# Four gates' 1x1 convolutions as one group of 16 small products, with mixing tiles shared by four gates

## The chip, the cores and the metric

The kernel runs on one core of a Trainium2 chip. The metric is the time of one launch on the device in microseconds (us). TensorE (PE in the profile) multiplies matrices into PSUM; VectorE (DVE), ScalarE (ACT) and GpSimd (POOL) do elementwise work; SyncE (SP) and GpSimd issue DMA transfers. Each engine has a queue of its own and takes its instructions in the order of the program.

## The reference

The input is x of 8 batch elements, 8 channels, 512 x 512, in float32. Two layers follow one another, each added to its own input. The second one, cut to what matters here:

```python
def layer0(x):                    # on group-normalized x: 4 x 8 Fourier modes
    ...
def _L1_conv_ref(x, ...):         # on group-normalized x
    grid = drive = x
    for _ in range(15):
        mapped = 3.9 * grid * (1.0 - grid)
        local = conv3x3_per_channel(mapped, K_local)
        grid = 0.85 * (0.7 * mapped + 0.3 * local) + 0.15 * drive
    cml_out = clip(grid, 0.0001, 0.9999)
    h = relu(conv3x3(x, Wp, bp))                      # 8 -> 128 channels
    nca_out = sigmoid(conv1x1(h, Wu, bu))             # 128 -> 8
    gin = concat([x, cml_out, nca_out], axis=1)       # 24 channels
    g = sigmoid(conv1x1(relu(conv3x3(gin, Wg1, bg1)), Wg2, bg2))
    return g * cml_out + (1.0 - g) * nca_out
```

The change concerns the last two lines, the gate: a 3x3 convolution from 24 to 8 channels, a 1x1 from 8 to 8, and the mixing.

## The kernel before

All batch elements go through one core, one after another, in a program written out by hand: `keep_order` fixes the order of the source on every engine. The loop works in turns (`turn`, `work`). A turn holds, for element b:

- two of the 15-step map's slots (`Slabs.convolve` L524 and `settle` L537/L543). A slab holds 4 x 32 rows of 4 channels; one step is 48 products of 32x32 tiles into a pair of PSUM tiles, two adding instructions on VectorE (L537) and two squares on ScalarE (L543). Its row renewals (L570, L571) are DMAs issued by GpSimd.
- up to two hidden rounds (`Hidden.round` L723), each four rows of the 3x3 into 128 channels, evicted by ScalarE (L729) and VectorE (L731); after two rounds the 1x1 of the hidden layer (`Hidden.point` L742) with the eviction of y (L749 on ScalarE or L751 on VectorE), and after four a sigmoid (L755) and a store of 16 rows.
- `Others`: the gates of element b - 1, and the spectral layer (layer 0) of element b + 1, in pieces.

PSUM is four tiles, `pairs`, of two banks each. A turn's `near` and `far` are two pairs each: the first slot and the first round use near, the second ones far, and the gate's and the hidden layer's products at the end of the turn use near again. After two rounds the list of pairs is reversed, so the next turn's first slot uses what was far.

A gate (`Gate`) is 12 rows of output; an element has 43. `load` brings `gin` (three DMAs of 384, 320 and 320 KB) and `mix` (three of 192 KB). `conv` (L793) is 12 products into one bank. GpSimd takes the difference d of map and hidden output (L798), VectorE adds the scaled input (L799) and evicts with relu (L803). One turn later `point` does the 1x1 as three products of 128x32 weights in another bank (L810), ScalarE the sigmoid (L814), GpSimd the product with d (L816). One more turn later `finish` adds on VectorE (L821) and stores (L828). Its call stands after each slot's adding instructions.

Tiles for gates and spectral inputs come from 20 slots of 1 MB that they share with the map (`Slots`); `shared.most` bounds how many they may hold: 5, or 8 in the first part of an element, or 3 around the middle and the end. In `feed`, which runs between the slots and the rounds of a turn, gates are loaded, up to two ahead, with two slots each; the spectral layer keeps up to four.

After the last element's loop a tail remains: that element's other 80 hidden rounds and its 43 gates, one a turn.

Of the kernel before, what the change touches and what calls it, by code (L numbers as in the profile page):

```python
# [35 lines left out]
F32 = mybir.dt.float32  # L36
# [30 lines left out]
AHEAD, PAUSE = 12, 6  # L67
# [50 lines left out]
def conv_layers(ctx: ExitStack, tc: tile.TileContext, a, out):  # L118
# [10 lines left out]
    class Slots:  # L129
# [16 lines left out]

        def drop(self, t):
            self.free.append(self.held.pop(id(t))[1])
# [47 lines left out]
    gpoint = load("w_g2", [P, GR * C])  # L196
# [118 lines left out]
    def layer0(e, bank):  # L315
# [89 lines left out]
        def close(g, mv):  # L405
# [4 lines left out]
            for c in (2 * g, 2 * g + 1):  # L410
# [3 lines left out]
                def store(c=c, xt=xt):  # L414
                    nc.sync.dma_start(
# [349 lines left out]
    class Gate:  # L765


        def __init__(self, e, first):
            self.e, self.first, self.r0 = e, first, min(first, N - GR)

        def load(self):

            r0, self.at = self.r0, now[0]
            self.gin = shared.take([P, 4, N], "gin")
            self.mix = shared.take([P, 4, N], "mix")
            for q, src in enumerate((self.e.xn, self.e.cml, self.e.nca)):
# [3 lines left out]
                    in_=view(src, r0 * C * N, [[N, rows * C], [3 * C * N, 4], [1, N]]),  # L780
                )
            for q, src in enumerate((self.e.xn, self.e.cml, self.e.nca)):
                nc.sync.dma_start(
                    out=self.mix[: GR * C, q],
                    in_=view(src, (r0 + 1) * C * N, [[N, GR * C], [1, N]]),
                )

        def conv(self, ps):

            gin, (x1, d, ng) = self.gin, (self.mix[: GR * C, q] for q in range(3))  # L790
            for n, (dx, lo, hi, at) in enumerate(SHIFTS):
                for j in range(4):
                    nc.tensor.matmul(  # L793
                        ps[32 * j : 32 * j + 32, lo:hi], gband[:, dx], gin[:, j, at : at + hi - lo],
                        start=(n == 0), stop=(n == 2), tile_position=(0, 32 * j),
                    )

            nc.gpsimd.tensor_tensor(d, d, ng, ALU.subtract)  # L798
            nc.vector.scalar_tensor_tensor(  # L799
                x1, x1, self.e.back[: GR * C, 1:2], ng, ALU.mult, ALU.add  # L800
            )
            shared.drop(gin)
            nc.vector.tensor_scalar(self.mix[:, 3], ps, b_g1, 0.0, ALU.add, ALU.max)  # L803

        def point(self, ps):
            mix = self.mix
            ps = ps[: GR * C]
            for j in range(3):
                at = slice(32 * j, 32 * j + 32)
# [339 lines left out]
```

## Time and profile before

| | |
|---|---|
| Median of 3 runs | 9484.28 us (9464.85 to 9497.41) |
| Profiled execution, its own time | 9485.99 us |
| Its span, first to last instruction | 9484.2 us |
| Mean granted TensorE clock | 0.985 |
| L524, the map's products | 103680 records, 3696.7 us busy |
| L793, the gates' 3x3 | 8256 records, 963.8 us busy in two rows of the table by form |
| L814 sigmoid | 344 x 677 ns |
| L798, L816 on GpSimd | 344 x 1290 and 344 x 1274 ns |
| L799, L821, L803 on VectorE | 344 x 954, 921 and 750 ns |

A matrix product in float32 shows as two records of a matmul and two of a weight load, so twice as many records as products stand in the profile. The time between the starts of two groups tells what a group costs TensorE, since records overlap. A row of the table of costliest groups gives line, engine, operation, output and input tiles, shapes and count; then busy time and the mean of one in ns; then how long the engine sat idle just before them, and what ended that.

### The profile page before, as it was taken

What the parts mean: (1) busy time and instruction counts of PE and PEld (TensorE: products, weight loads), DVE (VectorE), ACT (ScalarE), POOL (GpSimd) and SP (SyncE); (2) the same over time, 40 slices, a digit from 0 to 9 for tenths busy, and PEclk for the clock granted to TensorE, in tenths of its full rate; (3) what the DMA queues carried; (4) which work ended last, traced back from release to release, by engine and by line L of the source; (5) the groups of instructions that cost most, each with busy time, mean ns of one, the idle gap of its engine ahead of it and who ended that gap; (6) DMA issues with size and microseconds to landing.
All of it is one profiled execution on the core that took longest, in us unless ns stands there. A gap on an engine that the chain in (4) does not pass through costs nothing. (4 is left out here: it accounts for less than half of the span.)

```text
span 9484.2 us, 331791 instructions
## 1 busy us (share of the span) xinstructions
PE 9052.0 (95%) x148976; PEld 4062.8 (43%) x148976; DVE 5647.2 (60%) x5820; ACT 4078.4 (43%) x4285; POOL 3362.1 (35%) x4422
## 2 busy tenths in 40 slices
PE   6999999999999999999999999999999999988998
PEld 3444444444444444444444444444444444333433
DVE  5665566655665556655566555665566655545555
ACT  2444444444444444444444444444444444434432
POOL 3232334334333343433434343243433433444322
PEclk9999999999999999999999999999999999999999
DMA  4241365555655655655655556565575665675287
GB/s 151 83 128 37 95 170 138 144 138 141 154 151 140 142 132 147 166 132 133 158 134 161 144 118 169 126 162 141 117 181 134 162 138 125 144 164 132 65 207 192
DMA packets 698558, 1327.07 MB, mean 140 GB/s; under 512 B 146938, under 2 KB 152442, under 8 KB 669650
## 3 DMA queue, kind: packets, MB, share of 16 engines
q1 hardware_dynamic: 594432, 1249.10, 52.1%
q0 software_dynamic: 100352, 55.61, 2.9%
q8 instruction: 1171, 19.19, 0.9%
q14 instruction: 249, 2.04, 0.1%
q10 hardware_dynamic: 2354, 1.14, 0.0%
HBM read 977.48 MB, written 270.61 MB: 132 GB/s over the span
## 5 line engine op out<-in xcount | busy, mean ns | idle before, releaser
L524 PE MATMUL pair<-m,band 32*32 32x512 f32 x103680 | 3696.7, 603 | 164.2 <-issue 105.7
L543 ACT ACTIVATE m<-m 128x1024 f32<-128x1024 f32 x2016 | 2128.5, 1056 | 2425.9 <-DVE m L537 2358.8
L723 PE MATMUL pair<-cols,w_p 32*128 32x511 f32 (+1 forms) x24576 | 2854.9, 603 | 59.8 <-DVE m L537 16.4
L524 PEld LDWEIGHTS pair<-m,band 32*32 32x32 f32 x103680 | 1999.4, 103 | 1793.0 <-issue 1006.5
L570 POOL DMA_DIRECT2D m<-m x1568 | 864.1, 551 | 3929.1 <-ACT m L543 3853.4
L537 DVE SCALAR_TENSOR_TENSOR m<-pair,dO 128x1024 f32<-128x1024 f32 x1152 | 1356.6, 1220 | 1187.3 <-PE pair L524 1023.6
L723 PEld LDWEIGHTS pair<-cols,w_p 32*128 32x128 f32 x24576 | 1302.0, 186 | 1627.7 <-issue 1147.9
L537 DVE SCALAR_TENSOR_TENSOR m<-pair,dE 128x1024 f32<-128x1024 f32 x1008 | 1187.8, 1220 | 1106.6 <-PE pair L524 912.8
L731 DVE TENSOR_SCALAR h<-pair,b_p 128x1024 f32<-128x1024 f32 x1024 | 1313.3, 1283 | 870.2 <-PE pair L723 865.3
L729 ACT ACTIVATE h<-pair,b_p 128x1024 f32<-128x1024 f32 x1024 | 1141.4, 1115 | 894.4 <-PE pair L723 893.7
L742 PE MATMUL pair<-h,w_u 128*32 128x512 f32 x8192 | 1062.7, 611 | 42.4 <-ACT h L729 40.8
L793 PE MATMUL pair<-gin,w_g 128*32 128x511 f32 (+1 forms) x8256 | 963.8, 600 | 3.7 <-DMA gin<-nca 2.9
L816 POOL TENSOR_TENSOR mix<-mix 96x512 f32<-96x512 f32 x344 | 438.3, 1274 | 1336.2 <-ACT mix L814 1267.7
L571 POOL DMA_DIRECT2D m<-m x1568 | 844.9, 539 | 30.0 <-issue 25.9
L742 PEld LDWEIGHTS pair<-h,w_u 128*32 128x32 f32 x8192 | 245.2, 110 | 699.8 <-issue 347.3
L755 ACT ACTIVATE y<-y,b_u 128x512 f32<-128x512 f32 x256 | 185.1, 723 | 821.8 <-DVE y L751 821.8
L793 PEld LDWEIGHTS pair<-gin,w_g 128*32 128x32 f32 x8256 | 234.8, 110 | 683.0 <-issue 458.1
L798 POOL TENSOR_TENSOR mix<-mix 96x512 f32<-96x512 f32 x344 | 443.8, 1290 | 73.2 <-DMA mix<-nca 69.1
L547 POOL TENSOR_SCALAR dO<-dO 128x2048 f32<-128x2048 f32 x72 | 391.9, 5443 | 112.4 <-DVE m L537 111.4
L749 ACT COPY y<-pair 128x512 f32<-128x512 f32 x256 | 150.2, 587 | 637.8 <-PE pair L742 510.2
L516 POOL TENSOR_SCALAR dO<-dO,base 128x512 f32<-128x512 f32 x288 | 207.1, 730 | 580.8 <-DMA dO<-xn 502.6
L810 PE MATMUL pair<-mix,w_g 128*32 128x512 f32 x2064 | 370.3, 605 | 42.7 <-DVE mix L803 39.6
(89 smaller groups left out, 3280.9 us busy)
## 6 DMA issues: line engine op xcount, KB each, us to landing
gin<-xn SPq DMA_DIRECT2D x344, 384.0 KB
cols<-xn SPq DMA_DIRECT2D x256, 512.0 KB
x<-in_x SPq DMA_DIRECT2D x120, 1024.0 KB
gin<-cml SPq DMA_DIRECT2D x344, 320.0 KB
gin<-nca SPq DMA_DIRECT2D x344, 320.0 KB
dE<-xn SPq DMA_DIRECT2D x288, 256.0 KB
dO<-xn SPq DMA_DIRECT2D x288, 256.0 KB
mix<-xn SPq DMA_DIRECT2D x344, 192.0 KB
```

The lines of the kernel that those rows point to most:

```text
L524: nc.tensor.matmul(ps[h // 2][32 * t : 32 * t + 32, h % 2], band[at, self.channel(step - 1, h, t), dx], m[at, t, dx : dx + N], start=(n == ...
L537: nc.vector.scalar_tensor_tensor(u[:, at], ps[q], FLOOR, d[:, at], ALU.max, ALU.add)
L543: nc.scalar.square(u[:, at], u[:, at])
L570: nc.gpsimd.dma_start(out=view(tb, rb, dims), in_=view(ta, ra, dims))
L571: nc.gpsimd.dma_start(out=view(ta, ra + s, dims), in_=view(tb, rb + s, dims))
L723: nc.tensor.matmul(ps[g // 2][:, g % 2, lo:hi], w_p[p, dx, i % 2], self.cols[p, i // 2, at : at + hi - lo], start=(n == 0), stop=(n == 2), ...
L729: nc.scalar.activation(h[:, :2], ps[0], AF.Relu, bias=b_p)
L731: nc.vector.tensor_scalar(h[:, 2:], ps[1], b_p, 0.0, ALU.add, ALU.max)
L742: nc.tensor.matmul(ps[32 * g : 32 * g + 32], w_u[:, r % 4], h[:, g], start=(r == self.hs[0][0]), stop=(r == self.hs[-1][0]), tile_position ...
L793: nc.tensor.matmul(ps[32 * j : 32 * j + 32, lo:hi], gband[:, dx], gin[:, j, at : at + hi - lo], start=(n == 0), stop=(n == 2), tile_positi ...
L798: nc.gpsimd.tensor_tensor(d, d, ng, ALU.subtract)
L816: nc.gpsimd.tensor_tensor(d, d, mix[: GR * C, 2], ALU.mult)
```

## The change

Four gates make a `Quad`; eleven of them an element, the last of three gates. The four gates' 3x3 go one a turn as before, each with its own `gin` tile, but the four column groups of gate k are rotated by k (`to`), so that the relu results of four gates lie in different partitions; they are evicted into one tile `relu`, which takes the place of the first gate's `gin` (`swap`). The three mixing inputs are tiles `ng`, `d` and `x1` that all four gates share, of 128 partitions (four groups of 32, of which 24 hold results) and four gates; they are loaded once the fourth gate's `gin` has been, as slots come free, by 12 DMAs of 256 KB.

`blend` does the mixing for the four at once: one subtraction on GpSimd and two instructions on VectorE. `point` does the 1x1 of the four gates as 16 products of 32x32 weights, each in a tile of the array of its own, into all four banks of near; then two sigmoids on ScalarE and two multiplications on VectorE (on GpSimd before). `finish` adds half a quad at each call, so over two slots, and the quad is stored at the end of the turn by 12 DMAs.

`feed` moves from between the slots and the rounds to the end of the turn; loading the spectral input stays where it was (`fetch`). A gate loaded at the end of one turn may be convolved in the next. No new quad is begun from 18 slots ahead of the end of an element's first half of the map until 2 after it (`held`).

```diff
+AHEAD, PAUSE, HELD = 12, 6, 6
...
+        def swap(self, t, name):
+            tag = self.held.pop(id(t))[1]
+            new = wk.tile(t.shape, F32, tag=tag, name=name, bufs=1)
+            self.held[id(new)] = new, tag
+            return new
...
+    gpoint = load("w_g2", [P, 32])
...
         def conv(self, ps):
+            gin, quad = self.gin, self.quad
             for n, (dx, lo, hi, at) in enumerate(SHIFTS):
                 for j in range(4):
+                    to = 32 * ((j + self.k) % 4)
                     nc.tensor.matmul(
+                        ps[to : to + 32, lo:hi], gband[:, dx], gin[:, j, at : at + hi - lo],
+                        start=(n == 0), stop=(n == 2), tile_position=(0, to),
                     )
-            nc.gpsimd.tensor_tensor(d, d, ng, ALU.subtract)
+            if self.k == 0:
+                quad.relu = shared.swap(gin, "relu")
+            else:
+                shared.drop(gin)
+            nc.vector.tensor_scalar(quad.relu[:, self.k], ps, b_g1, 0.0, ALU.add, ALU.max)
+            quad.convolved, quad.at = quad.convolved + 1, now[0]
...
+    class Quad:
+        def load(self):
+            src = (self.e.nca, self.e.cml, self.e.xn)[len(self.mix)]
+            t = shared.take([P, 4, N], ("ng", "d", "x1")[len(self.mix)])
+            for j in range(4):
+                nc.sync.dma_start(
+                    out=t[32 * j : 32 * j + 32, : self.n],
+                    in_=view(
+                        src, (self.r0 + 1 + 3 * j) * C * N,
+                        [[N, 32], [GR * C * N, self.n], [1, N]],
+                    ),
+                )
+            self.mix.append(t)
+            self.loaded = now[0]
+
+        def blend(self):
+            n, (ng, d, x1) = self.n, self.mix
+            nc.gpsimd.tensor_tensor(d[:, :n], d[:, :n], ng[:, :n], ALU.subtract)
+            for k in (0, 2):
+                k1 = min(k + 2, n)
+                nc.vector.scalar_tensor_tensor(
+                    x1[:, k:k1], x1[:, k:k1], self.e.back[:, 1:2], ng[:, k:k1], ALU.mult, ALU.add
+                )
+            shared.drop(ng)
+            self.blended = True
+
+        def point(self, near):
+            n, relu, (_, d, _) = self.n, self.relu, self.mix
+            self.pointed = True
+            for k in (1, 3, 0, 2):
+                for j in range(4 if k < n else 0):
+                    at, to = 32 * ((j + k) % 4), 32 * j
+                    nc.tensor.matmul(
+                        near[k // 2][to : to + 32, k % 2], gpoint[at : at + 32],
+                        relu[at : at + 32, k], start=True, stop=True, tile_position=(at, to),
+                    )
+            for k in (0, 2):
+                k1 = min(k + 2, n)
+                nc.scalar.activation(
+                    relu[:, k:k1], near[k // 2][:, : k1 - k], AF.Sigmoid, bias=b_g2
+                )
+                nc.vector.tensor_tensor(d[:, k:k1], d[:, k:k1], relu[:, k:k1], ALU.mult)
+            shared.drop(relu)
+
+        def finish(self):
+            _, d, x1 = self.mix
+            k, k1 = self.shown, min(self.shown + 2, self.n)
             nc.vector.scalar_tensor_tensor(
+                d[:, k:k1], d[:, k:k1], self.e.back[:, 0:1], x1[:, k:k1], ALU.add, ALU.add
             )
+            self.shown = k1
+            if k1 < self.n:
+                return False
+            shared.drop(x1)
+            later(0, self.store)
+            return True
...
+            for quad in self.quads:
+                while not quad.gates and len(quad.mix) < 3 and shared.room() > kept:
+                    quad.load()
...
         point = rounds and e.hidden.n % 2 == 0
+        quad = others.point()
         gate = others.gate(near[0][:, 0])
-        others.spectral((far[0], far[1]) if gate else (near[0], far[0] if point else near[1]))
+        if gate or quad:
+            others.spectral((far[0], far[1]))
+        else:
+            others.spectral((near[0], far[0] if point else near[1]))
         if point:
             e.hidden.point(near[1][:, 0])
-        if not others.point(near[0][:, 1]):
+        others.blend()
+        if quad:
+            quad.point(near)
+        else:
             others.spectral([near[0] if gate or point else near[1]])
         tick()
+        feed()
         squares()
...
+            others.held = first.end - AHEAD - HELD <= at < first.end + 2
```

`Others.point` returns a quad whose gates are all convolved and whose mixing tiles are loaded, both by an earlier turn; `next_gate` gives the next gate to load, and no gate of a next quad before the quad in hand has its three mixing tiles.

## The prediction

> **What bounds the kernel now.** I read the page's busy times first, then the busy times by stage, then the timeline of one turn.
>
> ```profile
> PE 9052.0 (95%) x148976; PEld 4062.8 (43%) x148976; DVE 5647.2 (60%) x5820; ACT 4078.4 (43%) x4285; POOL 3362.1 (35%) x4422
> L810 PE MATMUL pair<-mix,w_g 128*32 128x512 f32 x2064 | 370.3, 605 | 42.7 <-DVE mix L803 39.6
> ```
>
> TensorE is busy 95% of the span; the products to be merged (L810, six records for each of 344 gates) have their own row. A busy share doesn't tell whether the work is dense, so the stages:
>
> ```profile
> 4640.00:5780.00 1140.00, 1115.98 (x18470) 502.13 (x18453) 698.40 (x719) 505.95 (x532) 411.07 (x531) 0.99 0.58 145
> 8070.00:8990.00 920.00, 819.28 (x15634) 359.15 (x15634) 480.70 (x461) 365.69 (x374) 397.86 (x520) 0.97 0.54 126
> 8990.00:9484.00 494.00, 455.12 (x3923) 160.22 (x3908) 252.08 (x236) 144.29 (x165) 108.27 (x86) 0.96 0.80 195
> ```
>
> Columns: window, length, busy time of PE, weight loads, DVE, ACT, POOL, granted clock, DMA share, GB/s. A middle element (first row) is 98% TensorE. The last element's loop (second) is 89%: other waits share the end there. The tail (third), where only hidden rounds and gates are left, is 92%, with DMA at 0.80. One turn of a middle element, TensorE alone:
>
> ```profile
> 3000.22 6.58 PE L524 MATMUL pair<-m,band 32*32 32x512 f32 x192
> 3006.73 5.43 PE L723 MATMUL pair<-cols,w_p 32*128 32x512 f32 x48
> 3012.08 2.78 PE L793 MATMUL pair<-gin,w_g 128*32 128x512 f32 x24
> 3014.68 1.90 PE L742 MATMUL pair<-h,w_u 128*32 128x512 f32 x16
> 3016.39 1.04 PE L810 MATMUL pair<-mix,w_g 128*32 128x512 f32 x6
> 3017.36 6.58 PE L524 MATMUL pair<-m,band 32*32 32x512 f32 x192
> ```
>
> Start to start, nothing is idle: 17.14 us. L810 holds TensorE 0.97. Turns without it (L742 at 3808.01, L524 at 3809.86) still spend 1.85 instead of 1.71 on L742, as the transition to L524 stays. So a removed group is worth 0.97 - 0.11 = 0.86 us. L524 puts 192 records into 6.51 us: 34 ns each, with 16 small tiles at work.
>
> The same turn on the other engines:
>
> ```profile
> 3003.63 2.36 DVE L537 SCALAR_TENSOR_TENSOR m<-pair,dO 128x1024 f32<-128x1024 f32 x2 [5.01 <-PE pair L524]
> 3005.90 0.74 DVE L821 SCALAR_TENSOR_TENSOR mix<-mix,back 96x512 f32<-96x512 f32 x1
> 3006.86 2.36 DVE L537 SCALAR_TENSOR_TENSOR m<-pair,dO 128x1024 f32<-128x1024 f32 x2 [0.22 <-issue]
> 3014.09 1.29 POOL L798 TENSOR_TENSOR mix<-mix 96x512 f32<-96x512 f32 x1
> 3016.65 0.69 DVE L751 TENSOR_TENSOR y<-y,pair 128x512 f32<-128x512 f32 x1 [0.89 <-PE pair L742]
> ```
>
> The first L537 pair ends at 3005.99, 0.74 us before hidden round 1 (3006.73) takes its banks. The second ends at 3009.22, 0.2 us before round 2 takes the others (about 3009.4). VectorE, idle 40% of the time, has under a microsecond of slack at these two points. Last, two lines that stretch:
>
> ```profile
> L799 DVE SCALAR_TENSOR_TENSOR mix<-mix,back x344: 733/739/4361, 1197.1 to 9464.4; 96x512 f32<-96x512 f32 x172
> L547 POOL TENSOR_SCALAR dO<-dO x72: 5360/5378/5792, 538.8 to 8947.7; 128x2048 f32<-128x2048 f32 x72
> ```
>
> ```profile
> 9457.48 1.84 DVE L799 SCALAR_TENSOR_TENSOR mix<-mix,back 96x512 f32<-96x512 f32 x1 [0.69 <-DMA mix<-nca]
> 9457.51 1.26 POOL L798 TENSOR_TENSOR mix<-mix 96x512 f32<-96x512 f32 x1 [1.51 <-DMA mix<-nca]
> ```
>
> L799 takes 0.74 us alone, 1.84 beside a GpSimd instruction of 1.26, and 4.36 at worst, beside L547's 5.38. L537, with one operand in PSUM, never shows it.
>
> [...]
>
> **The change, part by part.**
>
> *Products.* Removed: 344 groups, 0.86 each. Added: 88 waves (11 quads in each of 8 elements). A wave has 16 products, 32 records, 1.09 us at 34 ns. But it uses all four near banks, one of which the hidden 1x1 has just filled. Count from the start of L742: it ends at 1.71, its eviction (L751, or L749 on ScalarE) at 2.66. Products of k = 1 can go at once; k = 3 and k = 2 lie in that pair and wait until about 2.72. From there 24 records take 0.82, so the next convolution starts near 3.6: 1.9 instead of 0.11, or 1.78 a quad. Bounds: 1.0 (no wait) and 2.8 (the eviction late).
>
> *GpSimd.* L798 and L816 (eight a quad, 10.3 us) become one subtraction of 128x2048. Not in the trace; three bounds: 3.9 from L798 with 0.4 fixed, 4 x 1.29 = 5.2, [...] It is queued behind the turn's row renewals and starts where L798 did, at -0.6; it ends at 3.9. The next renewals come some 9 us later, so they aren't delayed.
>
> *VectorE.* L799 and L821 go (eight a quad at 0.95 and 0.92 mean, 7.5 us). Added: two mixings, two multiplications, two additions, each of 128x1024. L751 against L431 shows 0.53 for 512 more columns, so 1.27, 1.21 and 1.27: again 7.5 us. The amount stays; its place doesn't. With five slots I followed the tiles by hand: the third mixing tile is loaded when the third gate has freed a slot, so mixing and products fall in the same turn, every fourth turn. VectorE after L751 (2.66): mixing 1 runs at a sixth of its speed until GpSimd is done (3.9), ends at 5.0, mixing 2 at 6.2; the multiplications, whose sigmoids (two of 1.1, from 3.7) are done by 5.9, at 8.6. Queued behind them is the next L537 pair, due at 3.6 + 3.41 = 7.0. It ends at 11.0; round 1, due at 10.1, waits 0.9. Then the first addition (to 12.2), then the second L537 pair (to 14.6), while round 2 is due at 13.7: another 0.9. Together 1.85 a quad. With six slots (the start of an element), mixing comes a turn earlier: 0.5 there, 0.6 after the products, 1.1. While the spectral layer runs, its statistics sit in the same queue: 1 us more, an estimate from one piece's L431 (1.21) and two L433 (0.69 each). A delay under 0.7 costs nothing.
>
> *Small edits.* On ScalarE four L814 of 0.68 become two sigmoids of 1.1, off the path in a turn with rounds; in a turn without, the next L524 writes the same pair and waits some 2.4 us, which is in the last element below. A third spectral piece fits into turns without a wave: work moved, not changed. New quads aren't begun in ten turns around the middle of an element; by the same count of slots four or five quads fit before, seven after, eleven in all. One left over goes into the next element at no cost, after the last one at some 40 us (four turns of the tail). The swapped tile, `back`'s fourth buffer and the smaller weights: nothing.
>
> *DMA.* Mixing loads grow from 192 to 256 KB a tile and gate, 64 MB in all on 1327. Stores become 12 a quad instead of 4, so SP issues 8 more a quad, about 4 us in 68. A middle element has DMA at 0.58, so I take nothing; in the tail 2.23 MB a turn of 10.6 us (gin 1.05, mix 0.59, out 0.20, cols 0.26, nca 0.13) become 2.43, near 230 GB/s, against 252 in the best 20 us of the last element. Gate loads move from mid-turn to the end of the turn, past the stores and the mixing loads; the first gate of a quad then has some 13 us before its convolution for 1 MB. Nothing where DMA is at 0.58; bound: 3 us a quad.
>
> *Sum.* Elements 1 to 6 (258 gates, 66 quads): -258 x 0.86 = -222; waves +66 x 1.78 = +117; 42 quads at 1.85 = +78; 24 beside the spectral layer at 2.5 = +60: +33. Last element: many turns have no hidden 1x1, and L810 waits about 1 us for L803 (39.6 us in its row) and L524 for the sigmoid (14.4): -37 - 40 - 14 = -91; added 11 x (3.4 + 1.5) = +54; -37, of which I take half, -19, as TensorE is only 89% busy there. Tail: -38 x 0.86 = -33, +9.5 x 3.0 = +28, drain with 12 stores +5: 0. Total +14 on 9486 (span 9484.2, 1.8 around it; the median of the runs, 9484.3, is as good as equal): 9500.
>
> **The rivals.**
> - *The bursts are hidden* (VectorE's 40% of idle time speaks for it, the 0.2 us before round 2 against): the stalls of 78 + 60 fall away, and 15 each in the last two stages: -154, about 9335.
> - *The lock decides* (the other side). If GpSimd starts its subtraction late, behind a renewal or an L547, VectorE's two mixings and all that is queued behind them shift with it. From a start at about +1.5 instead of -0.6 each microsecond goes to TensorE; 2.5 us more in 77 quads is 190: 9690. For it: L547's 5.38 and L799's 4.36. Against it: L798 regularly starts at -0.6.
> - *Late gate inputs*: 3 us in 77 quads, 230: 9730. For it: the last-moment load and DMA at 0.75 in spectral stretches; against: L793 waited for DMA only 2.9 us in all.
> - *It isn't a wave*: the 16 products split around the eviction. That is in the forecast already; if the pairs are tracked by bank, only k = 2 waits, and 3.6 stays.
>
> **How the numbers follow.** Forecast 0.50 (9440 to 9560, by 0.7 us a quad either way), bursts hidden 0.20, lock 0.18, late inputs 0.12. For 8 in 10: half of the hidden case and a third of the two slow ones stay outside, which gives 9380 to 9630; the forecast's own range is 9440 to 9560. This kernel can tell 0.3% (28 us) from no change. Faster: 0.20 and 0.10 of the forecast, 0.30; same: 0.23 of the forecast; slower: 0.17 of it and 0.30, 0.47.
>
> **What would show it.** Right: the rows of L524 and L723 on TensorE wait for VectorE (their L537, or the new multiplications and additions ahead of it) some 150 us longer in all than before; the mixing instructions stretch well beyond 1.27; from the start of a hidden 1x1 to the next L524 there are about 3.6 us where a wave comes between. Wrong: turns after a wave without idle TensorE (hidden), mixing above 4 us in most quads (lock), or L793 waiting for gin by over 50 us (late inputs). A wave of over 2.8 us would make the sum wrong by itself.

## The result, and the profile after

The changed kernel takes 9821.32 us (median of 4 runs, 9802.62 to 9842.48), the kernel before 9476.11 us beside it: a ratio of 1.0362, 95% interval 1.0333 to 1.0392. That is 3.6% slower, 345 us, where the forecast was 9500 and its range ended at 9630. The profiled execution has a span of 9800.8 us against 9484.2, so 316.6 us are to be found in the two traces. The granted clock is 0.971 on average, against 0.985.

The page of the changed kernel, first the busy times, then four rows of the costliest groups. L524, L723, L793 and L742 of before are L531, L730, L795 and L749 here; L810's place is taken by L851.

```profile
PE 9099.6 (93%) x149664; PEld 4145.9 (42%) x149664; DVE 5730.6 (58%) x5660; ACT 4031.5 (41%) x4117; POOL 2863.6 (29%) x3822
...
L531 PE MATMUL pair<-m,band 32*32 32x512 f32 x103680 | 3786.5, 607 | 237.6 <-issue 158.5
...
L730 PE MATMUL pair<-cols,w_p 32*128 32x511 f32 (+1 forms) x24576 | 2976.7, 611 | 129.8 <-issue 50.3
...
L795 PE MATMUL pair<-gin,w_g 128*32 128x511 f32 (+1 forms) x8256 | 988.9, 612 | 90.9 <-DMA gin<-nca 71.7
...
L838 DVE SCALAR_TENSOR_TENSOR x<-x,back,ng 128x1024 f32<-128x1024 f32 (+1 forms) x176 | 294.4, 1713 | 88.4 <-DMA x<-xn 82.7
```

TensorE has less to do and is busy for longer: 9099.6 us instead of 9052.0. Two kinds of wait have grown: "issue", in which it waits for nothing that the profile shows, and gin by DMA. The same waits before (us in total, times, longest):

```profile
PE pair L524 <- issue: 105.7, 72, 3.7
PE pair L723 <- issue: 13.9, 11, 3.0
PE pair L793 <- DMA gin<-nca: 2.9, 2, 1.8
```

The busy times by stage, cut within some 3 us of where the same hidden round starts in both traces: the beginning, the elements up to the last one's loop, the last element's loop, and the tail. The columns are window, length, busy time of PE, weight loads, VectorE, ScalarE and GpSimd, granted clock, DMA share and GB/s.

```profile
0.00:1179.00 1179.00, 1055.84 (x17920) 506.98 (x17920) 702.22 (x797) 509.52 (x534) 365.00 (x600) 0.98 0.34 97
1179.00:8320.00 7141.00, 6794.74 (x112444) 3125.41 (x112440) 4301.18 (x4216) 3031.80 (x3094) 2126.22 (x2785) 0.98 0.61 148
8320.00:9246.70 926.70, 795.11 (x15373) 358.80 (x15370) 503.21 (x437) 352.18 (x346) 323.65 (x427) 0.94 0.57 131
9246.70:9800.00 553.30, 453.91 (x3938) 154.67 (x3936) 223.94 (x210) 137.96 (x143) 48.73 (x11) 0.91 0.81 189
```

Against the same four stages of before (1168, 6924, 905 and 487 us, with TensorE busy for 1050.96, 6745.15, 807.34 and 448.59):

| stage | longer by | forecast | idle TensorE before | idle after |
|---|---|---|---|---|
| beginning | +11 | 0 | 117 | 123 |
| elements to the last loop | +217 | +33 | 179 | 346 |
| last element's loop | +22 | -19 | 98 | 132 |
| tail | +66 | 0 | 38 | 99 |

Idle TensorE (length less busy time) grows by 268 us. A second part is the clock: it is granted at 1.0 or at 0.5 in both traces, 249 us of TensorE's busy time before and 468 after fall into stretches at 0.5, and half of that is counted as lost, 125 us and 234. With 3.3 us of one such stretch in it (4187.19 to 4190.60) a round of L730 takes 6.96 us from start to start, with 2.6 us of another (4258.87 to 4262.28) 6.60, where 5.36 are usual. Idle time and clock cost 378 us more; the work itself, at full clock, is 62 us less.

A turn with a wave, on TensorE, after which an ordinary turn follows:

```profile
4494.11 1.90 PE L749 MATMUL pair<-h,w_u 128*32 128x512 f32 x16
4495.94 1.57 PE L851 MATMUL pair<-relu,w_g 32*32 32x512 f32 x20
4497.03 0.61 PE L531 MATMUL pair<-m,band 32*32 32x512 f32 x1
4497.27 0.67 PE L851 MATMUL pair<-relu,w_g 32*32 32x512 f32 x12
4497.48 6.91 PE L531 MATMUL pair<-m,band 32*32 32x512 f32 x191
4504.32 7.07 PE L730 MATMUL pair<-cols,w_p 32*128 32x512 f32 x48
```

From L749's start to L730's are 10.21 us; without a wave (4513.91 to 4522.24) they are 8.33. The wave adds 1.88, and L730 itself takes 7.0 from start to start instead of 5.36, since VectorE is late with the map's results. On GpSimd and VectorE at the same time:

```profile
4493.65 4.55 POOL L835 TENSOR_TENSOR d<-d,ng 128x2048 f32<-128x2048 f32 x1
4496.68 3.81 DVE L838 SCALAR_TENSOR_TENSOR x<-x,back,ng 128x1024 f32<-128x1024 f32 x2
4500.41 2.35 DVE L860 TENSOR_TENSOR d<-d,relu 128x1024 f32<-128x1024 f32 x2
4502.69 2.34 DVE L544 SCALAR_TENSOR_TENSOR m<-pair,dE 128x1024 f32<-128x1024 f32 x2
```

All this is near the forecast. What the forecast doesn't have is a turn like the next, of 20.9 us instead of 16.3 or 17. TensorE, then the transfers that SyncE issues in it:

```profile
4249.84 6.19 PE L531 MATMUL pair<-m,band 32*32 32x512 f32 x170
4258.27 1.52 PE L531 MATMUL pair<-m,band 32*32 32x512 f32 x22 [2.24 <-issue]
4259.72 6.67 PE L730 MATMUL pair<-cols,w_p 32*128 32x512 f32 x48
```

```profile
4238.41 0.39 SPq L784 DMA_DIRECT2D gin<-nca  x1
4238.89 2.06 SPq L822 DMA_DIRECT2D ng<-nca  x4
4240.99 9.99 SPq L822 DMA_DIRECT2D d<-cml  x4
4251.98 0.54 SPq L587 DMA_DIRECT2D past<-m  x1
4253.31 4.12 SPq L822 DMA_DIRECT2D x<-xn  x4
```

TensorE stops in the middle of a convolution, after 170 of 192 records, and the profile shows no operand that it waits for. It stops again and again in turns whose transfers are the quad's three mixing tiles, 3 MB at once. What it waits for is its own instructions. The page lists a DMA queue of the kind "instruction", q8, with 1176 packets of 16 KB in this run. TensorE has 301,197 records (products, weight loads and 1869 others, most of them semaphores), so 256 for each packet, at 64 bytes. Number them from 0 in order of their starts. 390 start over 0.9 us after the one ahead, and 104 of these have a number of the form 193 + 256 n, where chance would give one or two. Each of the 104 starts 1.20 to 1.84 us after the n-th packet has ended, and of all 1175 records with such a number none starts less than 1.18 us after it. So each of these records is the first of those that a packet brings. In the turn shown one packet starts at 4246.11 and takes 1.90 us, where 1.2 are usual; the next starts at 4255.41 and ends at 4256.71, and 1.56 us later TensorE goes on, with record 193 + 256 x 519.

These stops at packets leave TensorE idle for 211 us; before, 73 of them left it idle for 118. They come where DMA is full. In the elements, 63 of 236 such first records stop TensorE where the DMA share in the 8 us ahead is above 0.9, and 1 of 346 where it is under 0.5.

### The profile page after: what moved, and what is told of

It reads as the page before. It is cut to its first block, busy times and chain, and to the rows that moved or that the text cites. A ratio compares the mean times of both kernels' runs of the same rounds, so it can differ in the third digit from the quotient of the medians.

```text
span 9800.8 us, 331322 instructions
## 1 busy us (share of the span) xinstructions
PE 9099.6 (93%) x149664; PEld 4145.9 (42%) x149664; DVE 5730.6 (58%) x5660; ACT 4031.5 (41%) x4117; POOL 2863.6 (29%) x3822
## 3 DMA queue, kind: packets, MB, share of 16 engines
q8 instruction: 1176, 19.27, 0.9%
## 5 line engine op out<-in xcount | busy, mean ns | idle before, releaser
L531 PE MATMUL pair<-m,band 32*32 32x512 f32 x103680 | 3786.5, 607 | 237.6 <-issue 158.5
L730 PE MATMUL pair<-cols,w_p 32*128 32x511 f32 (+1 forms) x24576 | 2976.7, 611 | 129.8 <-issue 50.3
L531 PEld LDWEIGHTS pair<-m,band 32*32 32x32 f32 x103680 | 2072.9, 103 | 1816.1 <-issue 1042.9
L730 PEld LDWEIGHTS pair<-cols,w_p 32*128 32x128 f32 x24576 | 1358.1, 189 | 1773.8 <-issue 1212.1
L749 PE MATMUL pair<-h,w_u 128*32 128x512 f32 x8192 | 1069.1, 616 | 59.8 <-ACT h L736 38.2
L795 PE MATMUL pair<-gin,w_g 128*32 128x511 f32 (+1 forms) x8256 | 988.9, 612 | 90.9 <-DMA gin<-nca 71.7
L803 DVE TENSOR_SCALAR relu<-pair,b_g 128x512 f32<-128x512 f32 x344 | 258.3, 751 | 563.4 <-PE pair L795 556.7
L795 PEld LDWEIGHTS pair<-gin,w_g 128*32 128x32 f32 x8256 | 241.4, 111 | 788.2 <-issue 595.5
L749 PEld LDWEIGHTS pair<-h,w_u 128*32 128x32 f32 x8192 | 248.4, 111 | 721.5 <-issue 418.7
L835 POOL TENSOR_TENSOR d<-d,ng 128x2048 f32<-128x2048 f32 (+1 forms) x88 | 392.1, 4456 | 521.1 <-DMA x<-xn 429.3
L756 ACT COPY y<-pair 128x512 f32<-128x512 f32 x256 | 149.8, 585 | 794.8 <-PE pair L749 541.1
L838 DVE SCALAR_TENSOR_TENSOR x<-x,back,ng 128x1024 f32<-128x1024 f32 (+1 forms) x176 | 294.4, 1713 | 88.4 <-DMA x<-xn 82.7
```

Of the source, the lines that this page charges most:

```text
L531: nc.tensor.matmul(ps[h // 2][32 * t : 32 * t + 32, h % 2], band[at, self.channel(step - 1, h, t), dx], m[at, t, dx : dx + N], start=(n == ...
L730: nc.tensor.matmul(ps[g // 2][:, g % 2, lo:hi], w_p[p, dx, i % 2], self.cols[p, i // 2, at : at + hi - lo], start=(n == 0), stop=(n == 2), ...
L749: nc.tensor.matmul(ps[32 * g : 32 * g + 32], w_u[:, r % 4], h[:, g], start=(r == self.hs[0][0]), stop=(r == self.hs[-1][0]), tile_position ...
L795: nc.tensor.matmul(ps[to : to + 32, lo:hi], gband[:, dx], gin[:, j, at : at + hi - lo], start=(n == 0), stop=(n == 2), tile_position=(0, to),)
L835: nc.gpsimd.tensor_tensor(d[:, :n], d[:, :n], ng[:, :n], ALU.subtract)
```

## The experiments

The theories that the expectations name: **S**, the bursts of mixing loads fill the DMA engines, and what TensorE needs (its instructions, the map's row renewals, gin) comes late; **V**, the bunch of six VectorE instructions behind each wave; **Q**, y's store behind a quad's 12 stores on SyncE's queue in the tail; and, later, **L**, the gates' own loads moved to the end of a turn. All ratios are against the kernel before on the same chip.

### Bursts on the kernel before

Twelve transfers of 256 KB from memory to memory were added to the kernel before, behind every fourth gate's loads (`b1_burst`) or three behind each gate's (`b2_even`):

```diff
+            if self.first // GR % 4 == 3:        # b1_burst; in b2_even always
+                for j in range(12):              # in b2_even range(3)
+                    nc.sync.dma_start(
+                        out=view(spare, j * 32 * 4 * 520, [[4 * 520, 32], [520, 4], [1, N]]),
+                        in_=view(self.e.xn, r0 * C * N, [[N, 32], [3 * C * N, 4], [1, N]]),
+                    )
```

> The kernel before with transfers that nobody waits for: behind every fourth gate's loads twelve more of 256 KB, from the normalized input to a scratch in memory, 3 MB at once as the changed kernel's mixing loads are. Theory S: TensorE's gaps after late fetch packets appear here too, at least as many as in the changed kernel, and the time rises by 100 us or more over before (9580 or above). Theory V: no more than 0.5 percent over before (under 9525).

> The same as the run with bursts, and as many bytes, but three transfers of 256 KB behind every gate. Theory S: since the bursts do the harm and not the bytes, at least 60 us faster than with bursts. If only the sum of bytes counts, both are as slow. Theory V: both within 0.5 percent of before.

The burst: 9650.47 us, 1.0182 [1.0161, 1.0203]. The same bytes, evenly: 9515.8 us, 1.0034 [1.0022, 1.0047]. By the pages 252 MB more cost 168 us when they come as 3 MB at once, and 271 MB more cost 34 when they come in small portions. The mean rate of DMA, 163 and 167 GB/s, can't tell the two. Stops at packets are 145 us in the first run and 117 in the second, so they are only a part of the burst's cost here; another is TensorE's wait for L749, the eviction of y, 82 us in the first, 31 in the second and 15 before.

### Parts of the changed kernel

`a1_drip` issues the mixing loads three at a time at two points of each turn. `a2_no_dve` leaves out the six VectorE instructions of a quad (mixing, product with d, addition), so the output lacks them. `a3_y_first` stores y ahead of the quad's outputs.

```diff
-            self.loaded = now[0]                 # a1_drip
+            for j in range(4):
+                others.drops.append((one, j))
...
+        def drip(self):                          # called twice a turn
+            for _ in range(3):
+                if self.drops:
+                    one, j = self.drops.popleft()
+                    one(j)
...
-                nc.vector.scalar_tensor_tensor(  # a2_no_dve, with the two below
-                    x1[:, k:k1], x1[:, k:k1], self.e.back[:, 1:2], ng[:, k:k1], ALU.mult, ALU.add
-                )
...
-                nc.vector.tensor_tensor(d[:, k:k1], d[:, k:k1], relu[:, k:k1], ALU.mult)
...
-            nc.vector.scalar_tensor_tensor(
-                d[:, k:k1], d[:, k:k1], self.e.back[:, 0:1], x1[:, k:k1], ALU.add, ALU.add
-            )
...
-            later(0, self.store)                 # a3_y_first
+            stores.append(self.store)
...
         for work in due:
             work()
+        while stores:
+            stores.pop(0)()
```

> The changed kernel with the same twelve mixing loads of a quad, but issued three at a time at two points of each turn, so that they are spread over two turns; tiles, slots and the order of all else stay. Theory S (the bursts of loads delay TensorE's own instruction fetch, TensorE runs dry, and its clock drops after it): the gaps that end about 1.5 us after a fetch packet fall from some 190 us back to the 115 of before, the clock rises from 0.971 towards 0.98, and the time falls by 100 to 150 us, to about 9700. Theory V (VectorE's work of four gates at once holds the next turn up): nothing changes, 9800 to 9840.

> The changed kernel without the six VectorE instructions of a quad: the mixing of the input, the product with the gate and the last addition are left out, so the output is only the difference of map and hidden output. Loads, products, sigmoids, GpSimd's subtraction and stores stay. Theory V: 88 quads are relieved of about 1.9 us each, the time falls by some 165 us to about 9655. Theory S: the turns of 20 us and more stay, the time falls by less than 80 us, to 9740 or above.

> The changed kernel with one swap of order: at the end of a turn the twelve stores of a quad are put behind the store of the hidden layer's y instead of ahead of it. Theory Q (in the tail the y store stands behind twelve stores on SP's queue, ScalarE can't refill the one y tile, and TensorE's hidden round waits for it): the 44 us that TensorE's hidden rounds waited for L756 go, the tail gets 40 us shorter, 9780 in all; the elements before the tail stay. Rival (the tail is bound by its transfers, which are as many): no change, 9810 to 9830.

Dripping: 9889.71 us, 1.0427 [1.041, 1.0443], slower still by some 68 us. Six a turn are 1.5 MB beside a gate's 1 MB, in two turns instead of one, and the stops at packets are as long as without dripping, 204 us against 211. What grows is TensorE's wait for y (L730 for L756, 119.1 us instead of 44.2). It speaks against S in the simple form that any spreading helps. No VectorE work: 9722.71 us, 1.025 [1.023, 1.027]: 98 us come back. Between the two profiled executions it is 68, and read at the same hidden rounds 63 of them lie ahead of the tail and 5 in it. V is real and not the main cause. y first: 9851.34 us, 1.0383 [1.0359, 1.0406]. Q falls: the wait for y goes (L730 for it 12.2 us instead of 44.2), but others take its place (L749 for VectorE 54.7 us instead of 20.8), and the tail is 550 us long instead of 554.

`a4_third` loads ng alone, d and x1 being computed from it; their tiles are taken but not filled, so the mixing is of the wrong inputs:

```diff
-            for j in range(4):
+            for j in range(0 if self.mix else 4):
                 nc.sync.dma_start(
                     out=t[32 * j : 32 * j + 32, : self.n],
```

`a5_all_off` is that, with the VectorE instructions left out and y first.

> The changed kernel with only one of a quad's three mixing tiles loaded (4 transfers of 256 KB instead of 12); the other two are computed from that one, so the loads of the map's output and of the input are left out and the output isn't the gate's. Instructions on all engines stay in kind, number and width. Theory S (bursts starve TensorE's instruction fetch): the gaps after late fetches fall to 115 us or less, the clock rises to 0.98 or more, and the time falls by 120 to 200 us, to between 9620 and 9700. Theory V (VectorE): no change, 9800 to 9840.

> The three suspects out at once: one mixing tile of three loaded, VectorE's six instructions of a quad left out, y stored first. What is left of the change is the wave of 16 products, its sigmoids and GpSimd's subtraction. If bursts, VectorE and the store order are all there is to the loss, what remains is the removed products (344 x 0.86) less 88 waves of 1.8: about 140 us faster than before, 9300 to 9400. Rival (something is still unnamed, in the wave itself or in the gates' new place in the turn): 9450 or above.

Eight of the twelve loads: 9502.36 us, 1.0022 [1.0012, 1.0031], 319 us less than with them. This is nearly the whole loss. Stops at packets are 131 us instead of 211. But with all three off it is 9453.56 us, 0.997 [0.9961, 0.998], and not the 1 to 2% that the removed products are worth. About 110 us were still open.

### The moved gate loads

`d1_late_gates` is the kernel before with one part of the change, gates' loads at the end of a turn, and nothing else:

```diff
         def transfers():
-            others.feed(t)
+            others.fetch(t)
...
         tick()
+        feed()
...
-            if not (self.loaded and self.loaded[0].at < now[0]):
+            if not (self.loaded and self.loaded[0].at <= now[0]):
```

> The kernel before with one part of the change alone: gates' inputs are loaded at the end of a turn (as in the changed kernel) instead of between its slots and its rounds, spectral inputs where they were; four gates still have four 1x1 and small mixing tiles. Before is 9478.6. If the moved gate loads cost what the changed kernel's convolutions waited for gin (72 us instead of 3), this kernel loses 50 to 90: 9530 to 9570, with L793's wait for DMA above 50 us. If the loss needs the mixing bursts ahead of the gate loads (theory: saturated DMA engines), it stays within 9465 to 9510, with L793's wait under 20 us.

9598.3 us, 1.0124 [1.0105, 1.0143]: 118 us, more than either side expected. TensorE's waits in it:

```profile
PE pair L524 <- issue: 101.9, 70, 4.0
PE pair L793 <- DMA gin<-nca: 89.2, 31, 9.6
...
PE pair L793 <- DMA mix<-xn: 10.2, 2, 5.4
...
PE pair L793 <- DMA dO<-xn: 5.6, 1, 5.6
```

Columns: us in total, times, longest. The issue wait is that of before (105.7); the loss is L793, which waits 105 us in all where it waited 3. So there are two mechanisms, and each can be had without the other.

### The wave without its tiles

`e1_one_late` keeps one mixing tile instead of three, and no VectorE work on it, so the output isn't mixed; that frees slots, so that its loads can go back to mid-turn in `e2_one_mid`. `e3_no_mix` has no mixing tile, and stores the sigmoid itself; `e4_even` loads the one tile in four parts, one with each gate, and so begins a quad only when two slots are free, as the tile is taken with the first gate; `e5_few_stores` is the third with 4 of 12 stores, so that two of three rows stay unwritten.

```diff
-            self.mix.append(t)
+            self.mix = [t, t, t]                 # e1_one_late, e2_one_mid
...
             others.fetch(t)
             for p in now_phases:
                 p.fetch(at)
+            others.feed(t)                       # e2_one_mid to e5_few_stores
...
                 g.load()
+                g.quad.part(g.k)                 # e4_even
...
+        def part(self, k):                       # e4_even
+            if k == 0:
+                self.ng = shared.take([P, 4, N], "ng")
+            nc.sync.dma_start(
+                out=self.ng[:, k],
+                in_=view(
+                    self.e.nca, (self.r0 + 1 + GR * k) * C * N,
+                    [[3 * C * N, 4], [N, 32], [1, N]],
+                ),
+            )
```

> The changed kernel with one mixing tile instead of three: ng alone is loaded (4 of 12 loads) and stands for d and x1, and the six VectorE instructions of a quad are left out, so the mixing isn't computed. The gates' inputs are still loaded at the end of a turn. It is the control of the next run and should be near the version with eight loads and six instructions left out (9453.6): 9420 to 9470, with L795 waiting for gin by 50 us or more.

> The run before with all loads of gates and quads back between the slots and the rounds of a turn, where the kernel before has its gate loads. If the moved gate loads are what eats the wave's gain (on the kernel before they alone cost 118): 60 to 130 less than the run before, 9310 to 9390, and almost no wait of L795 for gin. If the loss needs the large mixing tiles, and the wave itself is worth only some 30: within 25 of the run before, 9420 to 9470.

> As the run with one mixing tile and mid-turn loads (9456.6), with no mixing tile at all: nothing is loaded for the mixing, GpSimd's subtraction goes, and the sigmoid itself is stored, so the output is the gate's sigmoid without mixing. What is left of the change is the rotated groups, the wave of 16 products and the 12 stores. If bursts of mixing loads are what still makes TensorE wait for nothing visible (L531's issue wait 158 instead of 106): that wait returns to 90 to 115, and the time to the sum of the products, 9330 to 9390. If the wave or the stores bring it: issue wait above 140, 9420 to 9460.

> As the run with one mixing tile and mid-turn loads (9456.6), with the tile's 1 MB loaded in four parts of 256 KB, one with each gate's inputs, instead of at once. Its output lacks the mixing too. Same bytes. If the burst matters: L531's issue wait under 130 and 9370 to 9430. If bytes or the wave matter: 9445 to 9465, issue wait above 145.

> As the run without any mixing tile, with 4 of the 12 stores of a quad; two of three output rows are not written. If the stores' count on SyncE's queue matters in the loop or the tail: 30 or more below the run without mixing tiles. If not: within 15 of it.

| run | us | ratio to before | L531's issue wait | L795's wait for gin |
|---|---|---|---|---|
| `e1_one_late` | 9471.68 | 0.9992 [0.9983, 1.0001] | 164.3 | 15.8 |
| `e2_one_mid` | 9456.58 | 0.9975 [0.9963, 0.9987] | 158.0 | 11.0 |
| `e4_even` | 9283.45 | 0.9792 [0.9777, 0.9807] | 78.3 | 2.9 |
| `e3_no_mix` | 9238.29 | 0.9741 [0.9727, 0.9756] | 57.8 | 4.3 |
| `e5_few_stores` | 9240.58 | 0.9738 [0.9722, 0.9754] | 86.4 | 4.5 |

The first pair was expected to differ by 60 to 130 us and differs by 15. The traces show why. From the issue of a gate's first load to its convolution are under 14 us for 2 of 272 gates of the elements before, for 106 of 265 in `d1_late_gates` and 87 of 258 in the changed kernel, but only for 14 of 267 in `e1_one_late`, where free slots let gates be loaded further ahead. `a4_third` moves as few bytes as that run (1214 MB), but holds three tiles a quad, and there it is 91 of 269: the slots decide, not the bytes. The moved loads cost only while the slots are scarce, as they are in the changed kernel and in `d1_late_gates`.

One tile of 1 MB a quad, no more bytes in all than before (1214 MB against 1327), still leaves the issue wait at 158; the same tile in four parts, by another shape of transfer, brings 173 us, and stops at packets fall from 194 us to 86. Without any tile the kernel is 2.6% faster than before. That is no gain to be had, as the mixing and its loads are gone with it; but it shows that the wave, the rotated groups and the 12 stores aren't the loss. The number of stores does nothing to the time; the issue wait differs by 29 us between these two runs all the same, so smaller differences of it say nothing.

### Burst or shape

`e4_even` differs from its control in three things: the loads are spread, their shape is another, and a quad is begun only with two slots free. `f1_by_gate` changes the shape alone, in the complete changed kernel: four transfers of 128 partitions and one gate for each tile, instead of four of 32 partitions and four gates.

```diff
-            for j in range(4):
+            for k in range(self.n):
                 nc.sync.dma_start(
-                    out=t[32 * j : 32 * j + 32, : self.n],
+                    out=t[:, k],
                     in_=view(
-                        src, (self.r0 + 1 + 3 * j) * C * N,
-                        [[N, 32], [GR * C * N, self.n], [1, N]],
+                        src, (self.r0 + 1 + GR * k) * C * N,
+                        [[3 * C * N, 4], [N, 32], [1, N]],
```

> The changed kernel, complete, with each mixing tile loaded by gates (four transfers of 128 partitions and one gate) instead of by groups (four of 32 partitions and four gates). Same bytes, same number of transfers, issued at once as before. If it is the burst that costs: 9790 to 9850, as the changed kernel (9821), with the issue waits of L531 and L730 at 180 to 220 together. If the shape of the transfers is what made the run with an evenly loaded tile so much faster (9283 against 9457): 200 to 400 less than 9821, and issue waits below 140.

10571.76 us, 1.1139 [1.1115, 1.1164]. Neither side expected 750 us more than the changed kernel; but the waits of TensorE say what the shape does:

```profile
PE pair L795 <- DMA gin<-nca: 599.6, 54, 23.5
PE pair L339 <- DMA x<-in_x: 203.4, 18, 21.7
PE pair L749 <- DVE h L738: 167.4, 15, 20.4
PE pair L730 <- DVE m L544: 67.6, 9, 25.1
PE pair L531 <- issue: 65.3, 43, 3.7
...
PE pair L730 <- issue: 14.5, 9, 3.7
```

The two issue waits are 80 us instead of 209, and below the 120 of before, and the stops at packets 79 us instead of 211: with the same 3 MB issued together TensorE's instructions are mostly on time. The price is that all loads behind are late. The queue of SyncE during a quad's loads, and the busy times in this stretch, then those of the changed kernel in its own:

```profile
4404.51 6.10 SPq L822 DMA_DIRECT2D ng<-nca  x4
4410.65 10.84 SPq L822 DMA_DIRECT2D d<-cml  x4
4421.59 2.40 SPq L587 DMA_DIRECT2D past<-m  x1
4424.10 8.48 SPq L822 DMA_DIRECT2D x<-xn  x4
4433.38 1.76 SPq L653 DMA_DIRECT2D m<-past  x1
...
4436.84 0.65 SPq L784 DMA_DIRECT2D gin<-xn  x1
```

```profile
4412.00:4430.00 18.00, 18.00 (x304) 7.94 (x299) 8.49 (x8) 7.22 (x8) 2.19 (x5) 1.00 0.29 104
```

```profile
4240.00:4256.00 16.00, 16.00 (x266) 7.17 (x258) 8.03 (x7) 6.64 (x8) 4.37 (x8) 1.00 1.04 180
```

The last two columns are DMA's share and GB/s: 0.29 and 104 with the new shape, 1.04 and 180 with the old (packets' times overlap, so a share can pass 1). TensorE counts as busy in both, since the stop of the second comes after 4256. SyncE spends 2.11 us on one of these transfers on average, where it spent 0.44, and gin waits behind them.

How many engines one such transfer takes, no trace here shows. The share is that of 16 engines, so 0.29 is the time of 4.6 of them: the run with the new shape is one in which the burst leaves most of their time free.

A rival is that TensorE waits so long for gin in this run that its instructions have time to come. The traces speak against it. Take, in the elements, the first records of packets that fall within 10 us after a mixing load was issued, and of these the ones ahead of which TensorE was idle for under 0.6 us in 12: 42 of 209 stop it in the changed kernel, 7 of 308 here. Where the share is above 0.9 a stop is as likely as before, 23 of 83 against 63 of 236; there are fewer such stretches. Both runs together show the mechanism of S: what delays TensorE's instructions is a stretch with a DMA share above 0.9, and not bytes or a burst as such. What the 173 us of `e4_even` owe to the shape, to the spreading and to the free slots, these runs don't tell apart; its one tile, spread in the old shape, wasn't tried.

### The map's own loads

The kernel before also has bursts: the map's input loads, up to 16 of 256 KB in one go. `b3_ten_loads` and `b4_eight` allow ten and eight a turn, `c4_ten` is the changed kernel with ten, `c3_ten_off` is `a5_all_off` with ten.

```diff
-            while n - self.at >= -AHEAD and self.loads:
+            for _ in range(10):
+                if n - self.at < -AHEAD or not self.loads:
+                    break
```

> The kernel before with at most ten of the map's input loads (256 KB each) in one turn instead of as many as there are slots for; nothing is left out. Theory S: in the kernel before the late fetches stand behind these loads three times as often as chance has it, so spreading them brings the gaps after late fetches from 115 to 90 us or less and the time to 9440 to 9465. Rival (the gaps only move, or the later loads are waited for): 9475 or above.

> The kernel before with at most eight of the map's input loads in a turn, where ten gave 9458.6 and no bound 9478.6. If smaller bursts of transfers are what helped, eight gives at least as much: 9435 to 9460. If the ten was worth it only because it moved some loads apart from others, eight gives 9460 to 9490.

> The changed kernel with at most ten of the map's input loads in a turn. Theory of the bursts: the changed kernel has bursts of its own (12 mixing loads of 256 KB), which this leaves; it takes away only collisions with the map's input loads, worth 20 to 60: 9760 to 9800. If the map's loads have no part in it: 9810 to 9835.

> The changed kernel with eight of twelve mixing loads and the six VectorE instructions of a quad left out, y stored first (9453.6), and at most ten of the map's input loads in a turn. Of the d and x1 inputs nothing is loaded and the mixing isn't computed, so the output lacks it. If the rest of the loss of this version comes from the map's loads beside the gates' loads: 9400 to 9435. If it comes from the gates' own late loads, ten changes what it changed before, 20 at most: 9430 to 9455.

9458.62 us, 0.9977 [0.9967, 0.9986], and 9462.34 us, 0.998 [0.9971, 0.9989]: 20 us less than before, and the only complete kernels that beat both, by 0.2%. On the changed kernel it is 22 us (9799.33; 1.0333 [1.0313, 1.0354]), on the reduced one 23 (9430.31; 0.9951 [0.9933, 0.9968]). These two intervals overlap those without the limit, so the gains there are no more than likely. In the trace of before, 23 of the 73 stops at packets come within 10 us after one of these loads was issued, as 134 of all 1171 first records of packets do. The limit doesn't touch the change's own loss: stops at packets in the changed kernel stay at 211 us.

## Why the prediction was wrong

The step that failed is the one on DMA: "A middle element has DMA at 0.58, so I take nothing", and again, for the moved gate loads, "Nothing where DMA is at 0.58". The share is a mean over 1140 us. In the 16 us that matter it is 1.04, because the quad's loads fall together: 3 MB, with the next gate's 1 MB before or behind. Of the 217 us in the elements, the work of TensorE at full clock makes -19, where the sum has +33; idle time makes +167 and half speed +69, and for these the sum has nothing. Of the 167, waits for "issue" make 89 (stops at packets: 93 us before, 179 after) and waits for gin 36. Leaving out two of three mixing loads returned 319 us in all. The bytes were nearly right, 67.6 MB more by the pages where the prediction has 64.

Point by point:

- *Removed products at 0.86.* Right. A turn without a wave is now 16.29 us, before 17.14.
- *The wave at 1.78.* Right: 1.88 in the turn shown. The wave needed no eviction beyond the one forecast; it runs in two parts, of 20 and of 12 records, and the next convolution starts 3.4 us after the hidden 1x1, for 3.6 forecast.
- *GpSimd's subtraction, to end 4.5 us after its start.* Right, 4.55. The trace of before bears out only the bounds, 3.9 and 5.2, the first with L266's 0.37 us for 32 columns as the fixed part; between them 4.5 wasn't shown.
- *VectorE's burst.* Right in its place: L730 is late after a wave, by 1.6 us in the turn shown. Too large in its size: 138 us forecast for the elements, where leaving the instructions out returned some 30 between the two profiled executions (runs of one kernel differ by up to 40). The test of the forecast, 150 us more of waits for VectorE, failed: on L730 it is 21.0 us instead of 16.4. It was a poor test, as the 1.6 us of the turn shown don't appear as a wait either: TensorE's records overlap, and it counts as busy.
- *The lock.* What the traces show under this name is a VectorE instruction that takes longer beside one of GpSimd: L799 took 0.74 us alone and 4.36 beside L547's 5.38, which is the prediction's sixth of the speed. L537 took 1.20 to 1.23 us, beside L547 too (82 times). No run tested the cause. L838 is stretched, 1.71 us on average against 1.27 alone. Its median is 1.28, so most are not stretched, and the rival's sign, over 4 us in most quads, is missing. The rival of that name did not decide.
- *Late gate inputs.* The rival at a chance of 0.12, and its own sign, over 50 us of waits of L795 for gin, came true: 71.7. On the kernel before the move costs 118 us by itself. That the load moves to the end of a turn was seen; that scarce slots, and not bandwidth, leave it there until the last moment was not.
- *The tail at 0.* Mis-sized: +66. The terms were +28 for the waves, -33 and +5; TensorE's idle time there goes from 38 to 99 us, at a DMA share of 0.81 in both. None of it is stops at packets. With four of twelve mixing loads (`a4_third`) the tail is 465 us long instead of 554, and 487 before, so it is these loads; without the VectorE work it is 549. How they hold TensorE up there was not taken apart; of its waits in the tail, that for y (L730 for L756) grows from 14 to 44 us.
- *The clock.* No step had it. 109 us of the loss are work at half speed. In the changed kernel's trace the clock is granted at 0.5 in 116 stretches (64 before), 78 of them of 3.4 us. A gap of 2.5 us, which ends at 4186.26, is followed by one of these, with a mean granted clock of 0.78 from 4188 to 4194. Not every such gap is: of 26 gaps of 2 to 3 us that start over 9 us from any other above 0.3 us, 20 are followed by a stretch at half speed.

Of the rivals no one gave 9821. Late inputs at 9730 was nearest, and its mechanism is a part of the loss. What nobody had is TensorE's own instructions as a passenger on the DMA engines.

Between the two traces, 316.6 us apart, stops at packets make 93 us, half speed 109, and TensorE's waits for gin 69. What of the half speed belongs to which gap stays open, and so does the worth of each mechanism taken alone. They aren't additive: with fewer tiles both shrink, since free slots let gates load early.

## What to carry to other kernels

A mean DMA share says nothing of a burst (0.61 over the elements, 1.04 in the 16 us shown): before small transfers become few large ones, add up what one turn issues and look at the share in windows of some 10 us. Issue large loads in portions beside the work they serve, and look at the DMA share that a transfer's shape brings (0.29 or 1.04 here); a wait of TensorE for nothing, in the middle of a group and in a turn with much DMA, can be an instruction that hasn't arrived (104 stops here), and counting the records between such waits tells. And tiles that are held longer make other loads late, with no more bytes moved: under 14 us after the issue of their first load 91 of 269 gates are convolved in `a4_third`, 14 of 267 in `e1_one_late`.

## What the runs showed of the hardware

- TensorE's instructions come during the run, 19 MB in 1176 packets of 16 KB and 256 instructions each, on a DMA queue of their own. In 104 places TensorE stops at the first instruction of a packet until 1.20 to 1.84 us after the packet has ended, 211 us in all (118 before). Such a stop comes in 63 of 236 cases with a DMA share above 0.9 in the 8 us ahead, and in 1 of 346 under 0.5. No run changed the fetch itself. In three pairs of runs the stops differ: with loads at once and in portions 145 and 117 us (`b1_burst`, `b2_even`) and, the portions in another shape, 194 and 86 (`e2_one_mid`, `e4_even`); with the old shape and the new 211 and 79 (the changed kernel, `f1_by_gate`).
- In the stretches shown, mixing loads of 256 KB in four transfers of 128 partitions and one gate left the DMA share at 0.29, at 104 GB/s; in four of 32 partitions and four gates it was 1.04, at 180. SyncE needed 2.11 us to issue one instead of 0.44, on average.
- In stretches of 4 us with a DMA share above 0.95, `e4_even` moves 261 GB/s (270 stretches) and `e2_one_mid` 230 (451 stretches). Why was not tested.
